# Two graph layers on one core: GpSimd's sums of the next x^T later and in two parts, a longer delay in the kernel's own scheduler, the weight product's quarters moved, and a new order for the last pair

## The chip, the cores and the metric

One core of one Trainium2 chip. The time is the device time of one execution in microseconds (us); lower is better. The profile is one execution of each kernel; "span" is the time from its first to its last instruction. The record marks every execution used here as fast, at a mean granted TensorE clock of 0.97 to 0.99.

## The reference

64 batches of 256 nodes with 512 features pass two layers. Everything is float32.

```python
def layer0(x, adj, W):                       # W: 512 x 1024
    agg = einsum('bij,bjf->bif', adj, x) / maximum(adj.sum(-1, keepdims=True), 1e-6)
    return relu(einsum('bnf,of->bno', concatenate([x, agg], 2), W))
def layer1(X, adj, mask, Wqk, Wv):
    q, k = split(X @ Wqk, 2, -1); v = X @ Wv
    agg = einsum('bij,bjd->bid', adj, k * mask)
    w = mask * einsum('bid,bid->bi', q, agg) / sqrt(512)
    return softmax(w, axis=1)[:, :, None] * v
x = layernorm(x + layer0(x, adj, W0))
x = layernorm(x + layer1(x, adj, mask, Wqk, Wv))
```

## The kernel before

Batches are handled in pairs, 32 of them. While layer 0 of pair j runs, layer 1 of pair j-1 runs between its products. Each matrix product is done by a scheme of seven products (P1 to P7) of half-size blocks, P1, P2 and P5 by a second level of the same. This needs sums of blocks: of x^T (by GpSimd), of the layer's input transposed, x1^T (VectorE and GpSimd), of the adjacency (GpSimd) and of the gathered values (VectorE, tile `tv`). Other tiles that the profile names are `own` (the values that a layer norm works on), `agg` (what layer 1 gathers) and `z` (what layer 0 gathers). TensorE's results lie in eight PSUM banks; ScalarE copies them out (`act.copy`) and VectorE adds to them.

The two places that the argument turns on follow. First, the kernel's own list scheduler. Layer norms, softmax and the like are chains of steps for VectorE and ScalarE. While the program is written, a clock is advanced by each matmul, and after each unit of matmuls `tick` appends the steps that are due. It decides only the *order* in each engine's queue. On the chip the engine took its queue in that order and waited where it had to: the prediction's lines show ScalarE waiting 1.70 us for a layer norm's shift while a bank that it was to copy next lay ready.

```python
    vec = InOrder(tc, nc.vector, clock, lambda name, n: 0.07 + n / 960)     # n: elements written
    def step(chain):
        _, _, ready, steps = chain
        eng, work = steps.popleft()
        work()
        ready[0] = eng.free + 0.3 if steps and steps[0][0] is not eng else 0.0
        ...
    def tick():
        while True:
            for c in list(chains):
                if c[2][0] <= clock[0] and c[3][0][0].free <= clock[0] + room[c[3][0][0]]:
                    step(c)
                    break
            else:
                return
```

Second, the load of the next x^T and its sums, and one unit of the gather, which accumulates into the bank `u` after ScalarE has copied it and VectorE has added another bank:

```python
        def load_next():                         # called in the middle of layer 0's gather
            load_xT(j + 1)
            ...
            run_now(outer_sums(Xs[j + 1], gp))   # four sums of 128 x 512 elements: S1 to S4
            inner_sums(Xs[j + 1], gp, 0)         # four of 128 x 256
            inner_sums(Xs[j + 1], gp, 1)         # four of 128 x 128; they need S1
...
        def u3():                                # "e": S3 x T3
            twice(u, "S3", "T3", start=False)
            act.copy(r22, of(u))
            vec.tensor_add(r22, of(p5), r22)     # frees p5 for g3, "f"
            tick()
        def g3():                                # "f"
            twice(p5, "S4", "B22", start=False)
            ...
        def u4():                                # "g": waits for the copy of e
            twice(u, "A22", "T4", start=False)
            ...
```

## Time and profile before

| | before |
|---|---|
| time, median of 2 | 2079.47 us |
| span of the profiled execution | 2074.7 us |
| one pair in the steady part | about 61.5 us |
| matmuls of one pair at their unbroken spacing | 57.6 us |
| busy: TensorE, VectorE, ScalarE, GpSimd | 93%, 79%, 51%, 38% |

TensorE's busy share hides its gaps, because the modelled ends of its matmuls overlap (two 256-wide products are listed at 0.59 us, and the next starts 0.43 us after them). The spacing of their starts shows them. The prediction has the lines.

### The profile page before, as it was taken

How to read it: one execution, taken by the hardware profiler on the slowest of the kernel's cores; microseconds unless marked ns; L12 is line 12 of the kernel's file. 1: busy time of each engine (PE TensorE's matmuls, PEld its weight loads, DVE VectorE, ACT ScalarE, POOL GpSimd, SP SyncE). 2: the span in 40 equal slices, each digit the busy share in tenths (PEclk: the TensorE clock that was granted, in tenths of full speed). 3: DMA queues.
4: the chain of work that ended last, by engine and by line, in shares of the span. 5: the costliest groups of instructions: out<-in, count | busy, mean ns of one | idle time of the engine just before them, and what ended most of it. 6: DMA issues, size and time to landing. Idle time of an engine off the chain costs nothing.

```text
span 2074.7 us, 22478 instructions
## 1 busy us (share of the span) xinstructions
PE 1920.5 (93%) x6596; PEld 1245.7 (60%) x6596; DVE 1637.7 (79%) x2950; ACT 1061.2 (51%) x2565; POOL 795.5 (38%) x898
## 2 busy tenths in 40 slices
PE   8679999999999999999999999999999999999995
PEld 4356666666665666666666666666666666666662
DVE  3567787887787887788888778788778888778874
ACT  2335545555545555545555554555554555554443
POOL 2424333434334443434343424353433444343410
PEclk9789999999999999999999999999999999999997
DMA  5303333233434223433223433323343323343301
GB/s 173 81 24 105 94 80 89 81 96 97 107 70 104 69 90 97 107 87 87 74 86 96 106 87 87 78 91 97 98 107 69 102 71 90 97 107 87 77 27 40
DMA packets 389113, 182.15 MB, mean 88 GB/s; under 512 B 272128, under 2 KB 353664, under 8 KB 388992
## 3 DMA queue, kind: packets, MB, share of 16 engines
q1 hardware_dynamic: 388992, 180.72, 33.3%
q8 instruction: 53, 0.87, 0.2%
q14 instruction: 68, 0.56, 0.1%
HBM read 114.10 MB, written 34.06 MB: 71 GB/s over the span
## 4 chain that ended last, share of the span: by engine, by line
DVE 40%; PE 28%; SPq 9%; ACT 6%; DMA 6%; issue 5%; POOL 4%; DVEq 0%; ACTq 0%; POOLq 0%
PE bank L171 28%; SPq L176 9%; DVE tv L88 8%; DVE own L88 8%; DVE st L88 7%; DVE y L88 4%; POOL sa L88 4%; DVE x1T_s L88 3%; DMA x<-x 3%; DVE z L88 2%; DMA adj<-adj_t 2%; DVE agg L88 2%; DVE bank L88 2%; DVE mv L88 2%; ACT own L88 1%
## 5 line engine op out<-in xcount | busy, mean ns | idle before, releaser
L88 ACT COPY bank<-bank 128x256 f32<-128x256 f32 (+1 forms) x576 | 249.8, 437 | 284.2 <-PE bank L171 278.6
L88 POOL TENSOR_TENSOR sa<-adj 128x256 f32<-128x256 f32 x128 | 107.5, 840 | 400.3 <-DMA adj<-adj_t 265.4
L171 PE MATMUL bank<-w,x1T_s 128*128 128x512 f32 x512 | 260.3, 592 | 0.0
L88 ACT ACTIVATE own<-own,shift,rstd 128x512 f32<-128x512 f32 x256 | 205.0, 817 | 67.4 <-DVE shift L88 67.1
L171 PE MATMUL bank<-w,xT_s 128*128 128x512 f32 x512 | 230.2, 592 | 0.0
L88 POOL TENSOR_TENSOR xT_s<-xT 128x512 f32<-128x512 f32 x62 | 92.0, 1485 | 354.6 <-DMA xT<-x_t 272.6
L88 POOL TENSOR_TENSOR x1T_i<-x1T 128x256 f32<-128x256 f32 x64 | 51.2, 799 | 406.9 <-DMA x1T<-turn 388.1
L88 DVE TENSOR_TENSOR y<-bank,y 128x512 f32<-128x512 f32 x192 | 128.6, 683 | 96.2 <-ACT y L88 74.2
L171 PE MATMUL bank<-tv,sa 128*128 128x256 f32 x768 | 192.2, 379 | 1.7 <-ACT agg L88 1.3
L88 DVE BATCH_NORM_STATS2 st<-own 128x6 f32<-128x512 f32 x256 | 173.7, 678 | 4.4
L171 PEld LDWEIGHTS bank<-tv,sa 128*128 128x128 f32 x768 | 145.7, 190 | 49.7 <-issue 23.1
L88 DVE TENSOR_TENSOR bank<-bank,fifth 128x256 f32<-128x256 f32 x256 | 96.8, 423 | 93.0 <-PE bank L171 92.8
L88 ACT COPY y<-bank 128x512 f32<-128x512 f32 x192 | 109.5, 587 | 115.2 <-PE bank L171 106.9
L171 PE MATMUL bank<-t,x1T_s 128*128 128x512 f32 (+1 forms) x384 | 160.5, 527 | 0.0
L171 PE MATMUL bank<-t,xT_s 128*128 128x512 f32 (+1 forms) x384 | 158.8, 522 | 0.0
L171 PEld LDWEIGHTS bank<-w,xT_s 128*128 128x128 f32 x512 | 97.3, 190 | 95.1 <-issue 84.4
L88 DVE TENSOR_TENSOR z<-bank,z 128x512 f32<-128x512 f32 x96 | 66.0, 688 | 102.6 <-ACT z L88 63.0
L171 PE MATMUL bank<-t_i,xT_i 128*128 128x256 f32 x384 | 117.2, 388 | 27.6 <-POOL xT_i L88 11.7
L171 PE MATMUL bank<-t_i,x1T_i 128*128 128x256 f32 x384 | 118.5, 391 | 17.5 <-POOL x1T_i L88 8.9
L88 ACT ACTIVATE turn<-turn 128x256 f32<-128x256 f32 x128 | 52.6, 411 | 152.5 <-DMA turn<-adj 152.5
L171 PEld LDWEIGHTS bank<-t_i,xT_i 128*128 128x128 f32 x384 | 73.6, 193 | 94.9 <-issue 56.8
L171 PE MATMUL bank<-t,xT 128*128 128x512 f32 x256 | 125.5, 592 | 0.0
(133 smaller groups left out, 4298.9 us busy)
## 6 DMA issues: line engine op xcount, KB each, us to landing
xT<-x_t SPq DMA_DIRECT2D x64, 512.0 KB, 4.9
x<-x SPq DMA_DIRECT2D x64, 512.0 KB, 4.6
out<-own SPq DMA_DIRECT2D x64, 512.0 KB, 2.8
x1T<-turn SPq DMA_DIRECT2D x496, 64.0 KB, 2.3
adj<-adj_t SPq DMA_DIRECT2D x64, 256.0 KB, 3.0
turn<-adj SPq DMA_DIRECT2D x64, 256.0 KB, 4.9
row<-d SPq DMA_DIRECT2D x31, 256.0 KB, 4.7
wqk<-wqk_t SPq DMA_DIRECT2D x4, 512.0 KB, 5.7
```

The source lines that it names most:

```text
L88: return self.tc.keep_in_program_order(getattr(self.engine, name)(out, *args, **kwargs))
L171: tc.keep_in_program_order(nc.tensor.matmul(ps, a, b, start=start, stop=True, skip_group_check=True))
L176: return tc.keep_in_program_order(nc.sync.dma_start(out, in_))
```

## The change

Four things at once. (1) The scheduler waits 0.8 instead of 0.3 after a VectorE step, and 0.4 after a ScalarE step, before the chain's next step on another engine is due. (2) x^T is loaded later; the small sums and S1 follow the load, and S2 to S4 come at the start of the next pair. (3) Two quarters of the weight product leave the first pair's matmuls, and pair 0's norm is not flushed as a whole. (4) The last pair gets another order, with the scores before P3, and its output goes out in four parts.

```diff
-        ready[0] = eng.free + 0.3 if steps and steps[0][0] is not eng else 0.0
+        ready[0] = eng.free + (0.8 if eng is vec else 0.4) if steps and steps[0][0] is not eng else 0.0
...
-    run("m m m m n n n n", m=weight_product(0, wp[0]), n=weight_product(1, wp[1]))
+    for c in range(3):
+        run("m m m m", m=weight_product(c, (*wp, banks[3][0])[c]))
...
             load_adj(j)
+            run_now(late_sums)
+            late_sums.clear()
             sumsA[j] = adj_sums(j)
...
-            f = weight_product(2, pu[0]) + weight_product(3, pu[1])
-            run("i f k f i f k f i f k i f k f f", i=i, k=k, f=f)
+            run("i k i k i k i k", i=i, k=k)
...
-            run_now(outer_sums(Xs[j + 1], gp))
             inner_sums(Xs[j + 1], gp, 0)
+            rest = outer_sums(Xs[j + 1], gp)
+            run_now(rest[:1])
             inner_sums(Xs[j + 1], gp, 1)
+            late_sums.extend(rest[1:])
...
             run("e g f", **g)
+            run("m m m m", m=weight_product(3, pf[1]))
...
-            run("s s j a b s j c d s", s=s, j=jj, **g)
-            load_next()
-            run("j e k j g k f", j=jj, k=k, **g)
+            run("s s j a b s j c d s j e k j g k f", s=s, j=jj, k=k, **g)
...
-            run("k h h n k", k=k, h=h, n=n)
+            run("k h h", k=k, h=h)
+            load_next()
+            run("n k", k=k, n=n)
...
-            flush("norm")                       # after pair 0
... (last pair: order of the units)
-    run("i a i b i c i d e f g", i=inner("P1", X, W1, pw[1], u, b1), **g)
-    flush()
+    run("a b c i d i e i g i f m", i=i, m=m, **g)
+    flush("softmax", "adds")
-    run("m h i h m h i h m q i q m q q i", ...)
+    run("m h h m h h m q q n q q p p n p p", h=h, m=m, q=q, p=p, n=n)
... (scores, both softmax chains, then P3; norm and output in four parts)
```

More of the change, by code (lines that the diff above doesn't have):

```diff
@@ L166, in run @@
             units[name].pop(0)()
-    places = [None]
+    places, late_sums = [None], []
     def mm(ps, a, b, start=False):
@@ L560, in turn_last, with softmax_last @@
             copy(X.a[:, k, :, :, t].rearrange("p h e m -> p (h e) m"), ps[t].rearrange("p (c m) -> p c m", c=NF))
-    def softmax_last(j, k, w, ps):
-        wr = ps[0][:1, :N]
+    def softmax_last(k, w, ps):
+        wr = ps[:1, :N]
         for t in range(NT):
             tc.keep_in_program_order(nc.tensor.transpose(wr[:, t * P:(t + 1) * P], w[:, k, t:t + 1], ident))
-        top = small.tile([1, 1], F32, name="top1", bufs=2)
+        top, total = (small.tile([1, 1], F32, name=x, bufs=2) for x in ("top1", "total1"))
         vec.reduce_max(top, wr, axis=AX.X, negate=True)
         e = small.tile([P, HF], F32, name="fifth", bufs=3)[:1]
-        total = small.tile([1, 1], F32, name="total1", bufs=2)
         act.activation(e, wr, AF.Exp, bias=top, accum_out=total)
@@ L572, in softmax_last @@
         vec.tensor_scalar(e, e, total, None, op0=OP.mult)
-        for t in range(NT):
-            tc.keep_in_program_order(
-                nc.tensor.transpose(ps[1][:, t:t + 1], e[:, t * P:(t + 1) * P], ident[:1, :1]))
-        vec.tensor_copy(probs[j][:, k], ps[1][:, :NT])
+        return e
     def layer0(j, o, u, y):
@@ L761, in resnorm_kernel @@
             mask_adj(0)
-            flush("norm")
     j = NP - 1
     X = x1Ts[j]
-    run("f f f f", f=open1)
+    run("f f", f=open1)
     send_scores(j - 1)
+    run("f f", f=open1)
+    flush("norm", "mask")
     fetch_scores(j - 1)
-    flush()
     sumsM[j] = adj_sums(j)
@@ L778, in resnorm_kernel @@
     softmax(j - 1)
-    for pair in (pf, pw):
+    for pair in (pw, pf):
         fill(pair)
@@ L785, in resnorm_kernel @@
     g = gather(sumsM.pop(j), T, aggs[j], pw[0], o[1], o[0])
-    run("i a i b i c i d e f g", i=inner("P1", X, W1, pw[1], u, b1), **g)
-    flush()
+    i, m = inner("P1", X, W1, pw[1], u, b1), inner("P2", X, W1, pw[0], o, b2)
+    h, q = pairs(u, X, S2, W1["T2"], b6), pairs(u, X, S3, W1["T3"], b7)
+    p, r = pairs(u, X, A22, W1["T4"], b4), pairs(y, X, S4, W1["B22"], b3)
+    n = inner("P5", X, W1, pw[1], y, b5)
+    run("a b c i d i e i g i f m", i=i, m=m, **g)
+    flush("softmax", "adds")
     vs[j] = [late.tile([P, NT, F], F32, name="v", bufs=2) for _ in range(2)]
-    h, q = pairs(u, X, S2, W1["T2"], b6), pairs(u, X, S3, W1["T3"], b7)
-    run("m h i h m h i h m q i q m q q i", m=inner("P2", X, W1, pw[1], o, b2), h=h, q=q,
-        i=inner("P5", X, W1, pw[0], y, b5))
+    run("m h h m h h m q q n q q p p n p p", h=h, m=m, q=q, p=p, n=n)
     b8()
-    run("h h h h", h=pairs(u, X, A22, W1["T4"], b4))
     w = small.tile([P, 2, NT], F32, name="w", bufs=1)
     scale_scores(j, w)
-    run("h h h h", h=pairs(y, X, S4, W1["B22"], b3))
+    run("n n", n=n)
+    es = [softmax_last(k, w, pu[k]) for k in range(2)]
+    run("r r r r", r=r)
     probs[j] = small.tile([P, 2, NT], F32, name="probs", bufs=2)
     for k in range(2):
-        softmax_last(j, k, w, (pw, pu)[k])
-    finish(j)
+        for t in range(NT):
+            tc.keep_in_program_order(nc.tensor.transpose(pw[k][:, t:t + 1], es[k][:, t * P:(t + 1) * P], ident[:1, :1]))
+        vec.tensor_copy(probs[j][:, k], pw[k][:, :NT])
     flush()
+    x1 = owns[j]
+    for t in (1, 0):
+        for k in range(2):
+            o = x1[:, k, t:t + 1]
+            vec.scalar_tensor_tensor(o[:, 0], vs[j][k][:, t], probs[j][:, k, t:t + 1], o[:, 0],
+                                     op0=OP.mult, op1=OP.add)
+            stats, scale = layer_norm(o, small.tile([P, 1, 2], F32, name="mv"), 1)
+            run_now(stats + scale)
+            first(out[2 * j + k, t * P:(t + 1) * P], o[:, 0])
 def kernel(x, adj, nodemask, L0_gnn_W, L1_gnn_Wqk, L1_gnn_Wv):
```

## The prediction

> **What bounds the kernel now.** I read the page first, then TensorE's waits in the steady part, then one pair of batches in order of time, then the head and the tail. From the page:
> ```profile
> PE 1920.5 (93%) x6596; PEld 1245.7 (60%) x6596; DVE 1637.7 (79%) x2950; ACT 1061.2 (51%) x2565; POOL 795.5 (38%) x898
> ```
> TensorE leads, but 93% overstates it. In unbroken runs of the timeline a 512-wide instruction starts every 0.43 us and a 256-wide one every 0.215. One steady pair (about 61.5 us) has 64 of the first and 140 of the second: 64 x 0.43 + 140 x 0.215 = 57.6 us, so about 4 us of every pair are gaps. TensorE's waits, 118 us to 2003 us (about 30 pairs; us in total, times, longest):
> ```profile
> PE bank L171 <- ACT agg L88: 42.0, 29, 1.7
> PE bank L171 <- ACT bank L88: 41.6, 83, 1.1
> PE bank L171 <- POOL x1T_i L88: 8.9, 1, 8.9
> ```
> The first comes once per pair, always before the last product of the second gather; the third comes once in all. A wait also delays starts around it: the spacing shows 1.22 + 0.11 where the wait is 1.06. Over the steady part the gaps in the start spacing sum to 142 us: 49.7 at the agg wait, 13.2 before the fourth product of P1, 52 at two places of layer 1's P1 and P2, 9 at the x1T_i wait; the rest is scattered.
>
> The agg wait in order of time (other engines' rows between them left out):
> ```profile
> 1010.38 0.30 ACT L88 ACTIVATE rstd<-mv,eps 128x2 f32<-128x2 f32 x1 [2.11 <-DVE mv L88]
> ...
> 1013.20 0.15 DVE L88 SCALAR_TENSOR_TENSOR shift<-mv,rstd 128x2 f32<-128x2 f32 x1
> ...
> 1013.39 0.81 ACT L88 ACTIVATE own<-own,shift,rstd 128x512 f32<-128x512 f32 x1 [1.70 <-DVE shift L88]
> ...
> 1014.11 0.56 ACT L88 COPY agg<-bank 128x512 f32<-128x512 f32 x1
> ...
> 1014.73 1.13 PE L171 MATMUL bank<-tv,adj 128*128 128x256 f32 x4 [1.06 <-ACT agg L88]
> ```
> ScalarE is not full (51%): it is parked. The scaling of the layer norm stands in its queue ahead of the agg copy and waits for VectorE's shift; the bank copied had been ready since about 1011.2.
>
> VectorE is late there partly because GpSimd builds the sums of the next x^T in the same microseconds:
> ```profile
> 998.97 1.72 POOL L88 TENSOR_TENSOR xT_s<-xT,xT_s 128x512 f32<-128x512 f32 x1
> 999.48 1.76 DVE L88 TENSOR_TENSOR tv<-own 128x512 f32<-128x512 f32 x1
> ...
> 1046.68 0.68 DVE L88 TENSOR_TENSOR tv<-y,tv 128x512 f32<-128x512 f32 x1
> ```
> The same VectorE shape takes 1.76 beside GpSimd and 0.68 without it.
>
> The ends. Pair 0 to 1 (first two) and the last pair:
> ```profile
> 70.42 1.22 PE L171 MATMUL bank<-t_i,xT_i 128*128 128x256 f32 x2 [8.46 <-POOL xT_i L88]
> ...
> 85.53 2.07 PE L171 MATMUL bank<-t_i,xT_i 128*128 128x256 f32 x4 [9.23 <-ACT bank L88]
> ...
> 2038.30 1.22 PE L171 MATMUL bank<-t_i,x1T_i 128*128 128x256 f32 x2 [6.16 <-ACT bank L88]
> ...
> 2061.51 0.37 PE L575 MATMUL bank<-ident,fifth 1*128 1x1 f32 x2 [1.72 <-DVE fifth L88]
> ```
> The 9.23 and the 6.16 are queue order again: layer norm work was emitted whole in front of bank copies.
>
> **What the Trainium skill says.** "SBUF — State Buffer", section "SBUF: two separate sides": VectorE with two SBUF inputs and GpSimd take turns at a shared port pair, which is held for a whole instruction. The trace agrees: 1.76 is about one 0.68 plus the 1.27 of an undisturbed 512-wide GpSimd sum, with some overlap. So moving GpSimd work moves this delay, and removes it only where it lands beside VectorE work that reads PSUM or one input. "Perfetto Trace Analysis", section "Identifying Performance Opportunities", says consistent bubbles can mean too little SBUF or PSUM; here the bubble repeats in each pair, but the cause shown is queue order. "TensorE: Matmul & The Clock Gate", section on the HAM clock gate: an idle window of about 3.4 us drops the array to half clock. The trace agrees: after the 6.16 us wait, 2037 to 2042 ran at granted clock 0.50. A long wait removed thus also saves slow matmuls.
>
> **The change, part by part.**
>
> *Scheduler delay, 0.3 to 0.8 after VectorE and 0.4 after ScalarE.* No instruction is added; only queue positions move. I worked through the scheduler's own clock as coded. It charges the statistics by their six outputs, 0.15 for a pair that takes 0.68 + 0.18, so its VectorE clock runs ahead of the chip by over 2 us in a half norm. In a middle pair the last statistic is ready at 722.98 and the queue is tested at 723.69. With 0.3 the factor (rstd) goes in there, in front of P5's copies; with 0.8 (723.78) it goes behind them, at 724.55. Then the shift is ready at 725.77 instead of going in at 725.41; it goes in at the next test, 726.27, and the scaling at the earliest after the matmuls of the agg unit. So the agg copy precedes the scaling. Saved: the agg gap, 49.7 us. The same half microsecond puts the second P1 copy of the next pair in front of a scaling: most of 13.2, say 10. For the two gaps in layer 1's P1 and P2 the tests fall so that the factors stay where they are (706.19 is still before the test at 706.49): nothing. Sum 60.
>
> *x^T load and sums later and in two parts.* Per pair 4 GpSimd sums of 512 (1.27 to 1.72 us) and 8 smaller ones (0.45 to 1.2), about 12.6 us together, all unchanged. They ran from 994.7 to 1007.3; now the load is issued about 10 us later and they run some 10 us later. Contention leaves four tv sums and one add (excess over 0.68: about 1.0 each for three, 0.5 each for two, some 4 us) and falls on the two-input half of layer 0's norm, where I estimate about the same 4 us. VectorE's norm starts about 1 us earlier and ends about when it did. By itself worth nothing; it helps the statistics to be in time. The next pair's first products need the small sums at about +1081 and get them by about 1072: about 9 us of slack. In pair 1, x1T_i stood behind x^T sums in GpSimd's queue (the single 8.9); now it stands ahead: saved 9.
>
> *Weight product moved.* Eight units of 0.86 left pair 0's start, one of them already under a wait: 7 x 0.86 = 6.0, less some 0.7 of copy latency they had filled: 5.3. A quarter now lies in the idle 15.2 to 21.7 us, another (3.4) under the 8.46 wait. That wait also shrinks, since the small sums come first, and the 9.23 goes as pair 0's norm is no longer flushed whole. But VectorE then bounds: from norm to first layer 1 product it has about 21 us of sums, adds and weight sums left, after a norm ending near 79 instead of 86. I credit 9 in all.
>
> *Last pair.* Finishing pair 30 no longer blocks copies: 6.2, plus about 2 of half clock. Against it: one more fill pair ahead of the first product (0.9) and two stalls for agg copies in the tighter gather (0.7). Scores move before P3, so the two softmax chains, 5.5 us after P3 before, lie beside 3.4 of P3. But VectorE is in order: P5's adds (0.77 + 1.28) stand before the softmax and P3's adds after it, and each of the last four norms (about 2.4) waits for ScalarE before the next one: 9.7 instead of 9.0. From P4's end to ready probabilities I get 10.1 against 8.9, so the reordering gives nearly back what it hides, though 1.7 of P5 now lies inside it. Total 8.
>
> **Sum.** 60 + 9 + 9 + 8 = 86. I discount the 60 to 51, since removing a wait usually exposes another: 77, hence 2079.5 - 77 = 2002.5.
>
> **Rivals.** *VectorE becomes the bound.* It is busy 51 of 62 us in the pair from 1000 to 1062 and continuously so from 999 to 1025.5; its transposes feed 16 transfers (1025.65 to 1037.5), then x1T_i, which P1 needs at 1044.3. GpSimd had its first usable sum at 1040.2, so there are about 4 us of slack, some 2 for x1T_s. If contention in the norm is dearer than I estimate, x1T arrives late and TensorE waits on POOL or DVE: half of 60 is lost, total near 2035. For it: the continuous stretch. Against: the slack, and the contention taken from tv.
> *The agg wait only moves.* The scaling is then behind the agg copy but ahead of a v or own copy, and those sites grow: 2025 to 2040. Against: those products have 0.9 us or more of other matmuls between.
> *The norm is only late.* Longer delays push scalings into the next pair, where the flush emits them in a lump before P1's copies: another 0.5 us a pair, 2020. *Better than I say:* the two sites of 52 us shrink as well, 1980.
>
> **Range and chances.** The ends alone (26) give 1.2%. Faster by 2% means under 2038, needing only 16 of the 60, and the agg wait's order is worked out, not guessed: 0.89. Within 2%: 0.10. Slower: 0.01. Range 1980 to 2034.
>
> **What would show it.** Right: TensorE's wait on ACT agg below 10 us in total; no 8.9 us wait on x1T_i; ScalarE's wait of own for shift well below 67 us; tv<-own near 0.7 and the norm's two-input rows above 0.8; no wait over 4 us in the last 60. Wrong: TensorE waiting on POOL x1T_i or DVE x1T_s in each pair, or ACT bank waits above 60.

## The result, and the profile after

The changed kernel took 1988.09 us (1987.08 and 1989.09), and before 2079.47. The ratio is 0.9561, with a 95% interval of 0.9519 to 0.9602. Ratios here are the mean time of one kernel's fast runs over that of the other's fast runs of the same rounds, so they are not quite the ratios of the medians.

First, the engines' busy time in the page of the changed kernel:

```profile
PE 1911.8 (96%) x6596; PEld 1248.5 (63%) x6596; DVE 1576.4 (79%) x2952; ACT 1057.8 (53%) x2569; POOL 765.8 (39%) x898
```

The work is the same, but VectorE is busy 61 us less (1637.7 before) and GpSimd 30 us less. Their instructions had been held up by each other. TensorE's waits in the whole changed kernel (us in total, times, longest):

```profile
PE bank L171 <- ACT bank L88: 29.6, 52, 7.1
PE bank L171 <- DVE t_i L88: 8.0, 2, 4.6
PE bank L171 <- DVE agg L88: 7.5, 24, 0.6
...
PE bank L171 <- ACT agg L88: 0.2, 1, 0.2
```

The "agg wait", TensorE's wait for ScalarE's copy into the tile `agg` (43.3 in all before), is gone. There is a new one, on VectorE's agg add, 24 times. The 8.9 us wait for x1T_i in pair 1 is gone too. One steady pair in order of time, the same stretch that the prediction shows of before:

```profile
1023.40 0.30 ACT L88 ACTIVATE rstd<-mv,eps 128x2 f32<-128x2 f32 x1
...
1025.58 0.59 ACT L88 COPY agg<-bank 128x512 f32<-128x512 f32 x1 [1.65 <-PE bank L171]
...
1027.96 1.03 PE L171 MATMUL bank<-tv,adj 128*128 128x256 f32 x4
...
1028.77 1.52 ACT L88 ACTIVATE own<-own,shift,rstd 128x512 f32<-128x512 f32 x2 [1.74 <-DVE shift L88]
...
1029.47 0.66 DVE L88 TENSOR_TENSOR agg<-bank,agg 128x512 f32<-128x512 f32 x1
...
1030.18 1.13 PE L171 MATMUL bank<-own,sa 128*128 128x256 f32 x4 [0.33 <-DVE agg L88]
```

The agg copy now stands ahead of the scaling. ScalarE waits for the shift as long as before (1.74 against 1.70), but nobody waits for ScalarE meanwhile. The product that follows (`own,sa`) waits for VectorE, whose agg add stands behind the norm in its queue.

The groups of VectorE, first two of them before, then four in the changed kernel (busy us, mean ns of one, idle before):

```profile
L88 DVE TENSOR_TENSOR tv<-own,tv 128x512 f32<-128x512 f32 x64 | 94.9, 1483 | 1.2
L88 DVE TENSOR_TENSOR tv<-own 128x512 f32<-128x512 f32 x64 | 90.9, 1421 | 0.0
```
```profile
L88 DVE SCALAR_TENSOR_TENSOR own<-own,x 128x512 f32<-128x512 f32 x128 | 120.0, 937 | 3.3
L88 DVE SCALAR_TENSOR_TENSOR own<-z,rdeg,own 128x512 f32<-128x512 f32 x128 | 113.4, 886 | 0.0
...
L88 DVE TENSOR_TENSOR tv<-own,tv 128x512 f32<-128x512 f32 x64 | 45.0, 703 | 1.2
L88 DVE TENSOR_TENSOR tv<-own 128x512 f32<-128x512 f32 x64 | 44.3, 692 | 0.0
```

Before, the two norm rows (`own`) took 749 and 828 ns. The two tv rows alone gained 96.5 us in 32 pairs, about 3 per pair; the two norm rows lost 31, about 1 per pair.

The head and the end, changed kernel, in order of time:

```profile
64.69 1.20 PE L171 MATMUL bank<-t_i,xT_i 128*128 128x256 f32 x2 [2.60 <-POOL xT_i L88]
...
83.20 1.22 PE L171 MATMUL bank<-t_i,xT_i 128*128 128x256 f32 x2 [7.10 <-ACT bank L88]
...
1935.45 1.86 PE L171 MATMUL bank<-ones 1*128 1x512 bf16 x4 [4.30 <-DVE x1T L88]
...
1951.33 0.70 PE L171 MATMUL bank<-t_i,x1T_i 128*128 128x256 f32 x2 [0.93 <-ACT bank L88]
```

The first products of pair 1 wait 2.60 instead of 8.46 for x^T's small sums. The 9.23 wait is now a 7.10 one, later in the pair. The bank copy that ends it stands in ScalarE's queue behind the second half of pair 0's norm, for which ScalarE waits 3.88 us (VectorE's `mv`, until 80.61): the program still flushes that norm whole, in pair 1. In the last pair the 6.16 wait is 0.93. Part of what the ends gained is clock: the stretches in which TensorE was granted 0.50 add up to 44.4 us in the first pairs and 31.3 at the end before, and to 30.7 and 20.0 in the changed kernel.

To see where the time went I compared, pair by pair, the start of the first product of layer 0's gather in both traces (the "marks" from here on). The changed kernel is ahead there by 4.2 us in pair 0, 6.8 in pair 1, 17.0 in pair 2, 44.1 in pair 15 and 75.8 in pair 31, and by 87.4 at the end of the span. So the head gave 17.0, the 29 pairs between gave 58.8 (2.0 each), and the end 11.6. (The medians differ by 91.4, since the profiled run of before was some 3 us under its median.)

### The profile page after: what moved, and what is told of

It is laid out like the page before. It is cut to its first block, busy times and chain, and to the rows that moved or that the text cites.

```text
span 1987.3 us, 22612 instructions
## 1 busy us (share of the span) xinstructions
PE 1911.8 (96%) x6596; PEld 1248.5 (63%) x6596; DVE 1576.4 (79%) x2952; ACT 1057.8 (53%) x2569; POOL 765.8 (39%) x898
## 4 chain that ended last, share of the span: by engine, by line
PE 38%; DVE 32%; ACT 9%; DMA 6%; POOL 6%; issue 5%; SPq 5%; DVEq 0%; POOLq 0%; ACTq 0%
PE bank L171 38%; DVE own L88 11%; DVE st L88 5%; SPq L176 5%; DVE x1T_s L88 3%; DVE y L88 3%; DMA turn<-adj 2%; DVE tv L88 2%; POOL xT_i L88 2%; DMA xT<-x_t 2%; ACT y L88 2%; POOL sa L88 2%; ACT z L88 2%; DVE z L88 2%; ACT bank L88 2%
## 5 line engine op out<-in xcount | busy, mean ns | idle before, releaser
L88 POOL TENSOR_TENSOR xT_i<-xT 128x256 f32<-128x256 f32 x64 | 60.4, 944 | 579.3 <-DMA xT<-x_t 418.1
L88 ACT ACTIVATE own<-own,shift,rstd 128x512 f32<-128x512 f32 x256 | 201.8, 814 | 72.5 <-DVE shift L88 72.5
L88 ACT COPY agg<-bank 128x512 f32<-128x512 f32 x128 | 74.2, 580 | 112.7 <-PE bank L171 112.7
L171 PE MATMUL bank<-t,x1T 128*128 128x512 f32 x256 | 125.3, 592 | 0.0
L88 DVE SCALAR_TENSOR_TENSOR own<-own,x 128x512 f32<-128x512 f32 x128 | 120.0, 937 | 3.3
```

Of the source, the lines that this page charges most:

```text
L88: return self.tc.keep_in_program_order(getattr(self.engine, name)(out, *args, **kwargs))
L171: tc.keep_in_program_order(nc.tensor.matmul(ps, a, b, start=start, stop=True, skip_group_check=True))
```

## The experiments

My theory, *order*: what pays in the steady part is the longer delay, since it changes which instruction stands first in ScalarE's queue; moving GpSimd's work is worth little. The rival, *contention*: VectorE was late because GpSimd worked beside it, and the move of GpSimd's sums pays. Waits that are given for experiments are TensorE's between 200 and 1900 us; in that window the kernel before has 40.3 us on ACT agg and 37.8 on ACT bank. All outputs were correct. A "gap" is what the spacing of two starts has above the unbroken one; it takes in the slower starts just after a wait ("with restarts").

| run | time, median us | ratio to before |
|---|---|---|
| e1 delay only | 2033.26 | 0.9782 |
| e2 late sums only | 2038.79 | 0.9804 |
| e3 head and last pair only | 2065.84 | 0.9932 |
| e4 changed, delay 0.3 | 2020.83 | 0.9715 |
| e5 before, true charge | 2071.66 | 0.9947 |
| e6 changed, true charge | 2017.46 | 0.9701 |
| e7 changed, early load | 2006.66 | 0.9641 |
| e8 changed, whole sums | 2021.92 | 0.9721 |
| e9 changed, load still later | 1994.67 | 0.9591 |
| e10 whole sums, cut in two | 1995.46 | 0.9592 |
| e11 one swap in TensorE's order | 1977.91 | 0.9510 |
| e12 four edits together | 1952.90 | 0.9389 |

The kernel before, run beside them, had medians of 2079.8 to 2080.5. The changed kernel was run twice, in another round than these (ratio 0.9519 to 0.9602): where a run differs from it by some 10 us or less (e9, e11), the marks of the traces are given as well.

### e1: the delay alone

```diff
 # before
-        ready[0] = eng.free + 0.3 if steps ...
+        ready[0] = eng.free + (0.8 if eng is vec else 0.4) if steps ...
```

> The kernel before with the scheduler's delay alone changed (0.3 to 0.8 after VectorE and 0.4 after ScalarE). Theory, order: the agg copy then precedes the layer norm's scaling in ScalarE's queue whatever GpSimd does, so TensorE's wait on ACT agg falls from 43 to under 10 us and the time by about 50 to 60, to 2020 to 2030. Rival, contention: ScalarE waits because VectorE is late beside GpSimd, and another order only moves the wait; then 2060 to 2080, with the agg wait replaced by others of the same sum.

2033.26 us: 47 less. TensorE's waits:

```profile
PE bank L171 <- DVE agg L88: 20.6, 29, 1.2
PE bank L171 <- ACT bank L88: 20.4, 45, 0.8
```

The agg wait on ScalarE is gone, as the order theory has it, and the waits on copies of banks halved. But half of what was saved came back at once as a wait on VectorE's agg add, and the time is 3 us above the theory's range. In gaps, over the 29 pairs from 2 to 31: the agg gap of 49.7 us is gone and 28.3 stand at the agg add, a net of 21; the gaps before layer 0's P1 and in layer 1's P1 gave 27. So more than half of the gain comes from copies of banks, not from the agg copy. The time was not "moved only" either: the rival asked for 2060 or more. Both are partly right. The 0.4 has no part in it: a program with only that changed has the same order throughout, so it wasn't run.

### e2: the later load and the two parts alone

```diff
 # before, delay 0.3; the hunks with late_sums, rest and load_next of the change
```

> The kernel before with only the load of x^T later and its sums in two parts; delay 0.3 as before. Theory, order: only the 8.9 us wait of pair 1 goes, so 2065 to 2072, and TensorE's wait on ACT agg stays at 35 or more. Rival, contention: VectorE no longer shares its port in the sums of the gather (tv<-own back from 1.42 to 0.70 us), the statistics are in time, and the time falls to 2025 to 2045 with the agg wait below 15.

2038.79 us: 41 less, where I had expected 9. TensorE's waits:

```profile
PE bank L171 <- ACT bank L88: 38.1, 78, 1.0
PE bank L171 <- ACT agg L88: 12.2, 28, 1.1
```

With no step of the scheduler moved, the agg wait falls from 40.3 to 12.2. It is still there in every pair, so the order is unchanged; VectorE's shift simply comes earlier:

```profile
L88 DVE TENSOR_TENSOR tv<-own 128x512 f32<-128x512 f32 x64 | 44.2, 690 | 0.0
```

The contention theory holds here, and my theory falls on its second half. The waits on bank copies stay: those are the delay's.

### e3: the head and the last pair alone

```diff
 # before, with the hunks of the weight product, flush("norm") and the last pair
```

> The kernel before with only the weight product moved, pair 0's norm not flushed, and the last pair's new order. From the marks in the two traces (4.2 us gained at pair 0, 11.6 after pair 31's gather) I expect 2060 to 2066; both theories agree. If the ends are worth more than 25 us without the rest, the middle is worth less than the marks say.

2065.84 us: 14 less, as expected. By the marks it gains 4.3 us in pair 0, has 2.0 left in pair 2 and none (-0.15) in pair 31, so by itself the head's gain doesn't last: the wait for x1T_i in pair 1 is still there. What stays is the last pair's, 9.5 us between the traces (the two profiled runs are 9.4 apart, the medians 14).

The three gains sum to 47 + 41 + 14 = 102; together they gave 91. The marks show the overlap: over the 29 pairs e1 gains 45.5, e2 30.2 and the changed kernel 58.8. So 17 us of the two are the same, as both cut the agg wait, and on top of the delay the later load is worth 13.3 there.

### e4: the changed kernel with the old delay

```diff
 # after
-        ready[0] = eng.free + (0.8 if eng is vec else 0.4) if steps ...
+        ready[0] = eng.free + 0.3 if steps ...
```

> The changed kernel with the delay put back to 0.3. Theory, order: the middle gain goes, about 2030 to 2048, with TensorE's wait on ACT agg at 35 or more. Rival, contention: it keeps most of the gain, 1988 to 2003, with the agg wait below 15.

2020.83 us, between the two theories. Agg wait 11.8, bank copies 39.1: the same picture as e2. So on top of everything else the delay is worth 33 us. The larger part is the bank copies (39.1 to 19.8). The rest of the agg wait goes too, but of its 11.8 us 7.3 come back at the agg add.

### e5 and e6: the scheduler's charge for a statistic put right

```diff
-    vec = InOrder(tc, nc.vector, clock, lambda name, n: 0.07 + n / 960)
+    vec = InOrder(tc, nc.vector, clock,
+                  lambda name, n: 0.07 + (F if name == "bn_stats" else n) / 960)
```

(A statistic is `bn_stats`, which takes mean and variance of a row for a layer norm.) e5 is this in the kernel before:

> The kernel before, delay 0.3, with only the scheduler's charge for a statistic put right (the 512 elements read in place of the 6 written; 0.60 in place of 0.08). If the longer delay works by making up for that error, as my prediction says, this alone should give about what the delay alone gave: 2025 to 2045, TensorE's wait on ACT agg below 15. If the delay works for another reason (any shift of the queue would do), this gives less than half of it: 2058 to 2085.

2071.66 us: 8 less. TensorE's waits have no agg wait on ScalarE in the window and one of 1.3 us in the whole run, so at this place the undercharged statistic is what the longer delay makes up for. But ACT bank in the window rises from 37.8 to 59.5. One steady pair shows where: the last product of layer 0's P1 now starts 1.59 us late, and waits for a bank copy. A truer clock put steps into another place, which makes TensorE wait there in every pair. And the wait has a second cost: in 11 of the 29 pairs a stretch at half the clock follows it (start and end, length, busy time and count of TensorE, weight loads, VectorE, ScalarE and GpSimd, then the granted clock, DMA share and GB/s):

```profile
412.79 0.75 PE L172 MATMUL bank<-t_i,xT 128*128 128x256 f32 x2 [1.43 <-ACT bank L88]
```
```profile
413.30:416.70 3.40, 3.40 (x7) 2.02 (x7) 1.33 (x3) 1.60 (x4) 0.00 (x0) 0.50 0.61 116
```

The kernel before and e1 have no such stretch between 200 and 1880 us, and no wait in e5's window is longer than 1.43 us; so in this run the half clock came without the idle window of about 3.4 us that the prediction speaks of. Half of 11 x 3.41 us is 18.8 us, an estimate of what they cost; one of the four executions took 2062.77 at a mean clock of 0.975, the others 2071 to 2073 at 0.971. So by this estimate the new order by itself would give some 27 of the delay's 47 us. I had forecast the wait rightly and the time wrongly: it lies in the range of "any shift of the queue would do", for another reason than that one.

e6 is the same in the changed kernel:

> The changed kernel with the charge for a statistic put right as well, delays 0.8 and 0.4 kept. If both make up for the same error, nothing more is to be had: 1980 to 1998. If the queue order is still wrong in places (TensorE's 20 us on ACT bank, 16 at the agg add), 1960 to 1980.

2017.46 us, 29 slower than the changed kernel and outside both ranges. In the window it has no agg wait of either kind, but 56.2 us on ACT bank, 41.9 of them at that same product. What 0.8 does is not "correct the clock"; it gives an order that is good at several places at once, and a truer charge plus 0.8 gives another, worse one.

### e7 and e8: later load, or two parts?

```diff
 # e7: after, load_next() back in its old place; S2 to S4 stay in the next pair
-            run("s s j a b s j c d s j e k j g k f", s=s, j=jj, k=k, **g)
+            run("s s j a b s j c d s", s=s, j=jj, **g)
+            load_next()
+            run("j e k j g k f", j=jj, k=k, **g)
 # e8: after, the later load with the sums whole, large ones first
-            inner_sums(Xs[j + 1], gp, 0)
-            rest = outer_sums(Xs[j + 1], gp)
-            run_now(rest[:1])
-            inner_sums(Xs[j + 1], gp, 1)
-            late_sums.extend(rest[1:])
+            run_now(outer_sums(Xs[j + 1], gp))
+            inner_sums(Xs[j + 1], gp, 0)
+            inner_sums(Xs[j + 1], gp, 1)
```

> The changed kernel with the load of x^T and the first part of its sums put back to their earlier place; the other three sums stay in the next pair. If the place of GpSimd's work beside the sums of the gather is what the later load is worth, tv<-own goes back above 1.0 us and the time to 2005 to 2025. If the split alone carries the gain (its three large sums no longer run there), within 10 us of the changed kernel, 1985 to 1998.

> The changed kernel with the sums of x^T whole again, in their old order, behind the later load. In the trace GpSimd runs both parts without a break in the same place of the pair, so the split by itself should be worth only the head, where the small sums are waited for: 1988 to 1996. If the split matters in each pair, by 0.5 us or more, over 2003.

e7: 2006.66 us (1997.55 to 2009.31), 19 more than the changed kernel; tv<-own is at 1.06 us again, and the wait on the agg add is 21.4 in place of 7.3. As expected.

e8: 2021.92 us, 34 more. Here I was wrong: I had taken the split for a matter of the head alone. The same GpSimd work runs without a break in the same place in both; only its order differs. (In the program S2 to S4 come with the next pair, but in GpSimd's queue nothing stands between: S2 starts at 1029.51, as the last small sum ends, in the changed kernel.) In order of time, e8:

```profile
1044.03 1.60 POOL L88 TENSOR_TENSOR xT_s<-xT_s,xT 128x512 f32<-128x512 f32 x1
1044.54 1.64 DVE L88 SCALAR_TENSOR_TENSOR own<-own,x 128x512 f32<-128x512 f32 x1
1045.59 1.71 POOL L88 TENSOR_TENSOR xT_s<-xT 128x512 f32<-128x512 f32 x1
...
1047.89 1.64 DVE L88 SCALAR_TENSOR_TENSOR own<-own,x 128x512 f32<-128x512 f32 x1
```

and the group of that VectorE instruction with TensorE's wait:

```profile
L88 DVE SCALAR_TENSOR_TENSOR own<-own,x 128x512 f32<-128x512 f32 x128 | 144.6, 1130 | 3.3
```
```profile
PE bank L171 <- DVE agg L88: 37.2, 29, 1.9
```

With the large sums first, each add of the norm stands behind a 1.27 us instruction of GpSimd, and the agg add behind the norm comes late. With the small ones first, the norm meets mostly short instructions, and most of the large ones run after the agg add.

### e9: the load still later

```diff
 # after
-            run("k h h", k=k, h=h)
-            load_next()
-            run("n k", k=k, n=n)
+            run("k h h n k", k=k, h=h, n=n)
...
-            run("h h a n b q d q n c q e q p n g p f p", ...)
+            run("h h a n b", h=h, n=n, **g)
+            load_next()
+            run("q d q n c q e q p n g p f p", n=n, q=q, p=p, **g)
```

> The changed kernel with the load of x^T and its first sums another 3.9 us of matmuls later. If TensorE's remaining wait (agg add of VectorE, 7.5 us, with its restarts 16) comes from GpSimd holding the port beside the norm's first half, it goes and the time falls to 1968 to 1980. Rival: the small sums then come too late for the next pair's first products (they had about 6 us of slack), TensorE waits on POOL xT_i in each pair, and the time rises above 1995.

1994.67 us, 7 more than the changed kernel. The two ratios (0.9591 and 0.9561) lie within the error of the second, but the marks agree: it is 5.9 us behind at pair 31. Neither guess held. The wait on the agg add is 6.4 (7.3 in the changed kernel), and there is no wait on xT_i. own<-own,x takes 0.96 us, so the norm still meets GpSimd. The gaps show where it lost, not why: in front of layer 1's first product they are 5.4 us over the 29 pairs, 0.9 in the changed kernel. The cause stays open.

### e10: one hold of 1.27 us or two of 0.7

```diff
 # e8, for GpSimd only
-        return [(eng, lambda: eng.tensor_add(a(S1), a(A21), a(A22))), ...
+            def halves(to, op, c, d):
+                for k in range(2):
+                    gp.tensor_tensor(*(X.block(s, slice(k, k + 1)) for s in (to, c, d)), op=op)
```

> The kernel with whole sums (2021.9 us) with each 512-wide sum on GpSimd cut into two of 256. If what matters is how long one GpSimd instruction holds the port (a VectorE instruction waits for one such hold), the row own<-own,x falls from 1.13 to below 0.98 us, the wait on the agg add from 37 to below 20, and the time to 1992 to 2008. If what matters is how much GpSimd work lies beside the norm, own<-own,x stays above 1.05 and the time within 8 us of 2022 (GpSimd's work grows a little).

1995.46 us, 26 less than e8. The group of the norm's add, and the wait:

```profile
L88 DVE SCALAR_TENSOR_TENSOR own<-own,x 128x512 f32<-128x512 f32 x128 | 115.8, 905 | 3.3
```
```profile
PE bank L171 <- DVE agg L88: 8.8, 23, 0.7
```

GpSimd is busy longer (790.2 us against 770.2, in 124 more instructions), and yet VectorE loses less. So here it is the length of one GpSimd instruction that counts, not the amount of its work. This is what "SBUF — State Buffer", section "SBUF: two separate sides", of the Trainium skill says of the shared port pair: it is held for a whole instruction. The same section limits the hold to VectorE instructions with two SBUF inputs or in a two-port mode. The runs agree: the statistics, with one input, took 0.678 us before and 0.677 in all of after, e8 and e10, with GpSimd moved beside them, while own<-own,x went from 0.749 to 0.937, 1.130 and 0.905.

### e11: one swap in TensorE's order

```diff
 # after
-            run("k h h", k=k, h=h)
+            run("h k h", k=k, h=h)
```

> The changed kernel with one swap in TensorE's order: the first product of P6 in front of the third of P2, which waits 0.5 us and more in each pair for ScalarE's copy (20 us with restarts). If the copy is merely late by less than the 0.86 us now put in between, the wait goes: 1965 to 1975. Rival: P6 itself waits for ScalarE's copies of q out of the same bank, or the wait moves to the fourth product of P2: 1983 to 1992.

1977.91 us, 10 less than the changed kernel (9.3 at the mark of pair 31). The 20 us gap in front of P2's third product is gone, but the gain stops at half: the wait on the agg add grew from 7.3 to 12.3 (probably as VectorE had less time to catch up; not tested). This is between my two guesses.

### e12: a version that beats both kernels

```diff
 # after, with "h k h" of e11, the halves of e10, and
-            run("h h a n b q d q n c q e q p n g p f p", ...)
+            run("h h a n b q d q n c q e q p n g p p f", ...)
 # last four norms: the next add goes between a norm's factor and its shift
             vec.scalar_tensor_tensor(o[:, 0], vs[j][k][:, t], ...)
+            run_now(rest)
             stats, scale = layer_norm(o, ...)
-            run_now(stats + scale)
-            first(out[...], o[:, 0])
+            run_now(stats + scale[:1])
+            rest = scale[1:] + [(None, lambda ...: first(out[...], o[:, 0]))]
```

> The changed kernel with four edits together: the swap of e11, the large sums on GpSimd cut in two of 256, the last product of the second gather one P4 product later, and the last four norms interleaved. From e11 (1977.9) I expect the wait on VectorE's agg add (12.3 us, about 19 with restarts) to go for the most part and 1.5 us at the end: 1955 to 1968. If the agg add is late by more than the 0.86 us put in between, or the scores fall behind and the waits move to x1T: 1968 to 1980; over 1988 would say that one of the edits costs more than all of them save.

1952.90 us (1950.81 to 1953.43), ratio 0.9389 (0.9376 to 0.9401): 35 less than the changed kernel and a little better than forecast. TensorE's only wait left in the steady window:

```profile
PE bank L171 <- ACT bank L88: 6.7, 17, 0.7
```

How the 35 us divide among the four edits is not shown, beyond e11's 10 and that of 36 between the traces 32.7 are gained by the mark of pair 31, which leaves at most 3.3 for the last norms.

## Why the prediction was right, and where its steps were not

The time lies in its range, 14 us under its middle. That the steady part came out near its sum (51 forecast, 58.8 measured) is in part luck: the delay, forecast at 51, gives 45.5 there alone (e1), and the later load, forecast at nothing, adds 13.3. By its own steps:

- **What bounds the kernel.** Held. Summing start spacings over the same parts of the changed kernel, the steady part's gaps fell from 142 to 71 us, and the time there by nearly as much.
- **Scheduler delay: "Saved: the agg gap, 49.7 us", and 10 before P1.** Both old gaps are gone. The mechanism held: the scaling goes behind the agg copy, and it did so in e1 with nothing else changed. The size was off when taken alone: 16 us (with restarts) came back at the agg add, in e1 even 28. That VectorE's add would take the place of the copy is a wait I had not named. (The agg wait stands before the last product but one of that gather, `tv,adj`, and not before the last, `own,sa`, as the prediction has it.)
- **"For the two gaps in layer 1's P1 and P2 ... nothing."** Half wrong. Of 52 us 38 are left. The P2 gap stayed, but the P1 gap fell from 26 to 11, because one factor of the earlier layer norm did move behind a copy. The 706.19 took the statistics where they stood before. The scheduler's clock, logged while the program is built with the new delay, has them one test later, at 705.63 in place of 704.77; so the first factor is due at 706.88, after the test at 706.49, and the second falls behind P1's copies.
- **The discount from 60 to 51, "since removing a wait usually exposes another".** Its reason came true, 16 us at the agg add. What made up for it are the 14 us that the gaps of P1 and P2 lost against the forecast, and the later load, without which 28 come back instead of 16 (e1).
- **x^T load and sums: "By itself worth nothing."** This step failed. Alone it gave 41 us (e2), 9 of it the wait in pair 1 that I had listed apart. The mis-sized term is the contention that "falls on the two-input half of layer 0's norm, ... about the same 4 us": the tv rows gained 3 us per pair and the norm rows lost 1. (The terms listed for the gather are a little large too: in that pair the five excesses over 0.68 sum to 3.5 us, with two near 1.0 and not three.) And the sum of busy time is not what decides. In e8, with the sums whole, the norm rows lost 1.6 per pair, still less than the tv rows gained; yet its 29 pairs gain only 28.9 us, less than the 45.5 of the delay alone, because the agg add behind the norm comes late. The order and length of the sums (e8, e10), which I had called unchanged work, decide whether the later load pays.
- **Pair 1's x1T_i and the head: 9 + 9.** Measured 17.0 at pair 2: 6.8 at the mark of pair 1, then 10.2. "The 9.23 goes" was wrong: 7.10 are left, since pair 0's norm is flushed in pair 1 instead. Of the head, e3 shows that it doesn't last without the load moved.
- **Last pair: 8.** Measured 11.6. The 6.16 wait went (0.93), but a 4.30 wait for x1T came in front of the last pair, where I had said that none over 4 would be left; after it TensorE ran from 1936 to 1941 at a granted clock of 0.50.
- **The rivals.** "VectorE becomes the bound" and "the norm is only late" did not come; "the agg wait only moves" came in part, to another engine than I said. "Better than I say, 1980" is nearest, for its stated reason only in part.
- **The checks.** Two named signs were wrong: the wait of 4.30 in the last 60 us, and ScalarE's wait of own for the shift did not fall (67.1 to 72.5 us). The wait is as long; it only stands where nothing that TensorE waits for is behind it.

## What to carry to other kernels

Where an engine with spare time is waited for, look at what stands ahead of the wanted instruction in its queue and let the work that may be late go behind it; then look at once for the engine that is waited for next. Where GpSimd and VectorE both read two SBUF tensors, shorten GpSimd's instructions, or put its short ones first, before trying to move its work away. A scheduler's constant that was found by trial is a choice of order, and a truer cost model need not give a better one.

## What the Trainium skill lacked or had wrong

- "SBUF — State Buffer", section "SBUF: two separate sides", has the exclusive hold. It does not say that cutting GpSimd's own instructions shortens what VectorE loses to them: cutting GpSimd's 512-wide sums in two cost GpSimd 20 us of busy time and gained 26 us of run time (e8 to e10: 2021.9 to 1995.5), as the norm's add fell from 1.13 to 0.905 us.
- "Perfetto Trace Analysis", section "Identifying Performance Opportunities", gives missing buffer space as a cause of consistent bubbles. It lacks queue order: a bubble of 1.06 us in each pair went with no buffer added, by an order alone (e1: the agg wait on ScalarE from 40.3 us to none, though 20.6 came back as a wait on VectorE).
- No page read says that a wait can stay as long and cost nothing once another instruction stands ahead of it (67.1 us of waits before, 72.5 after, in a kernel 91 us faster).
